# Products of the sampling weights one group further ahead, and the first tables' work in another order

## The chip, the cores and the metric

The kernel runs on one core of a Trainium2 chip. The metric is the device time of one execution, in microseconds; lower is better. Before the change the median of three runs is 1502.04 us (1500.31 to 1502.71).

## The reference, cut to what matters

Eight images x of 128 channels and 64 by 64 pixels, float32, go through two layers; each adds its output to its input.

```
x = x + relu(batchnorm(deform_conv(groupnorm(x))))       # layer 0
x = x + moe_conv(groupnorm(x))                           # layer 1
...
om   = conv3x3(x, off_w) + off_b                         # 27 channels: 18 offsets, 9 masks
py   = off_y + row - 1 + ky;   px = off_x + col - 1 + kx # per pixel and tap
val  = bilinear(x, py, px) * sigmoid(mask)               # 4 corners, weights (1-ly)(1-lx), ...
out  = einsum('bckhw,ock->bohw', val, w) + b
```

Layer 0, where the change lies, samples the normalised image at nine displaced points for each pixel and multiplies the samples with a 3 by 3 weight. Layer 1 mixes four 3 by 3 experts with weights chosen per image, and is untouched.

## The kernel before, in words

The function dense() does layer 0. All offsets of this input are under two pixels, so a sample is a sum over 5 by 5 neighbours, with a "tent" weight in y times one in x. The kernel turns the bilinear sampling into matrix products.

**Tiling.** An image is eight bands of eight rows, so there are 64 bands. In x a band is 15 tiles (NCOL) of four columns, handled in five groups (NGR) of three tiles. The pixels of a tile and its surround, 8 by 8 in each of two halves of the band, lie on the 128 partitions of xt.

**Work of one band g.** load_x and load_y fetch rows of the distance table in x (tabx, into one of three x_wts) and of the tent table in y (taby, into one of three y_wts), most of them by DMA from GpSimd's queue (lines 746 and 727): ten DMAs, 1.9 MB. spread (765, 768, 771) turns the distances into tents on ScalarE and clips them on VectorE. weights(n) (850) is the product s of the x and y weights for group n, counted over all bands, on VectorE; the pool a6 has five such buffers. pick (780) and pixels (809, 812) copy and transpose the normalised pixels into xt; share (823) copies the overlapping halves of xt, in four pieces on VectorE, ScalarE and SyncE's DMA. sample(n) (866, 876) multiplies xt with s on TensorE and copies the samples from PSUM on ScalarE. close(g) (892 to 899) fills the edges of the band's samples on VectorE. conv(g) (915, 923) runs the nine taps of the 3 by 3 product for the rows of band g and stores the result.

**Order.** The order is written out by hand: nothing is reordered, and each engine takes its instructions as the program emits them. Step g of the main loop emits, for the five groups q, first weights(5g+q+AHEAD) with AHEAD = 4 and then sample(5g+q); at q = 1, between them and the next, put_off(), which emits the statistics of the last convolution (996) and close(g-1). Then come the taps of conv(g-1). Between taps stand the pixels and spreads of band g+2, the loads and pick of band g+3, and ticks, which advance the tables of a coming image. So the first four products of a band are emitted in the step before, and its fifth at the head of its own step. load_x(g+3) writes the buffer that the products of band g read, so it waits for the fifth.

**Tables.** tables(b) is a generator that makes the tables of image b: normalisation, the offset convolution (392, 458), a store of its result by rows and columns to DRAM (525, 532), loads of it in another layout (570, 556), distances (616 to 631), the tents and masks (641 to 678), and stores to tabx (596) and taby (668). For image 0 it runs at the head with nothing beside it. Lines 535 to 541 pick and transpose the pixels of bands 0 and 1 there, between the offset convolution and the tables, and line 542 negates dw_sb. The first bands' tables are then stored ahead of the rest, and load_x(0) and load_y(0) follow them on several queues. The tables of image 1 (called later) are begun inside step 0.

**Clears.** The three y_wts tiles are set to zero once (262), since their loads fill only the parts that carry weights.

Of the kernel before, what the change touches and what calls it, by code (L numbers as in the profile page):

```python
# [65 lines left out]
def deform_moe_conv(  # L66
# [113 lines left out]
    def dense():  # L180

        with ExitStack() as st:
# [77 lines left out]
            y_wts = [a1.tile([P, T, 3, W, 3], F32, name=f"ywts{i}") for i in range(3)]  # L260
            for t in y_wts:
                nc.gpsimd.memset(t, 0.0)

# [10 lines left out]
            def pause(n):  # L274
                for _ in range(n):
                    yield
# [34 lines left out]
            def tables(b):  # L311
# [159 lines left out]
                if b < 2:  # L471
# [13 lines left out]
                    yield from block(0)  # L485
                    nc.vector.tensor_tensor(even, even, taken(0), ALU.add)
                    yield from block(3)
                    nc.vector.tensor_tensor(odd, odd, taken(3), ALU.subtract)
# [47 lines left out]
                if b == 0:  # L536
                    for g in range(2):
                        pick(g)
                        for _ in pixels(g, turn_odd=not g):
                            pass  # L540
                    pick(2)
                    nc.scalar.activation(dw_sb, dw_sb, AF.Copy, scale=-1.0)
                nc.vector.tensor_reduce(
                    most[:, b : b + 1], omr, AX.X, ALU.max, apply_absolute_value=True
                )
                yield from pause(8 if b == 1 else 16)
                by_row = rowwise[b].rearrange("(t k u) h w -> k h t u w", t=3, k=3)
# [13 lines left out]
                for k in range(3):  # L561
                    lo, hi = max(0, k - 1), min(H, H + k - 1)
                    places = [(slice(lo, hi), slice(lo + 1 - k, hi + 1 - k), k)]
                    if k == 2:
                        places.append((slice(0, 1), slice(0, 1), 0))
                    if k == 0:
                        places.append((slice(H - 1, H), slice(H - 1, H), 2))
                    for outs, parts, v in places:
                        for t in range(2):
                            nc.sync.dma_start(  # L570
                                out=raw_off[parts, v, t].rearrange("p (u w) -> p u w", u=3),
                                in_=by_row[k][outs, 2 * t],
                            )
                        by_column.append((k, outs, parts, v))
                if b:
                    yield from pause(27)
                for k, *where in by_column:
                    turned_in(nc.sync if b or k == 0 else nc.gpsimd, k, *where)
                if b == 0:
                    for piece in range(4):  # L580
                        share(1, piece, MOVES[piece])
                yield from pause((50, 17)[b] if b < 2 else 35)
# [116 lines left out]
                store_x(0, 2, nc.gpsimd)  # L699
                load_x(0, nc.gpsimd)  # L700
                for i in (0, 1, 2):
# [3 lines left out]
                for i in (3, 0, 4, 1, 2):  # L705
                    masked(i)
                    store_y(i, 1, soon)
                for k in range(Q):
                    for h in range(2):
                        load_y(0, k, (nc.sync, nc.gpsimd, nc.scalar, nc.gpsimd)[k % 4], (h,))  # L710
                store_x(2, 4, nc.scalar)
                store_y(0, NR, slice(4 * T, H))
                store_x(4, NROW, nc.sync)
                for _ in statistics(1):
                    pass
                for tiles in ((NCOL, NCOL + 1), (0, 3), (3, 9), (9, NCOL)):
                    spread(0, tiles)
# [71 lines left out]
            def pixels(g, turn_odd=False):  # L789
# [14 lines left out]
                for c0 in range(0, NCOL if turn_odd else EVEN, 4):  # L804
                    n = min(4, NCOL - c0)
                    pt = ps_c.tile([P, 4, P], F32, name="pt", tag="pc")
                    for c in range(c0, c0 + n):
                        one = picked[:, c] if c < EVEN else picked_odd[:, c - EVEN]
                        nc.tensor.transpose(  # L809
                            pt[:, c - c0], one.rearrange("p h x y -> p (h x y)"), ident  # L810
                        )
                    nc.scalar.copy(xts[g][:, c0 : c0 + n], pt[:, 0:n])  # L812
                    yield
# [152 lines left out]
            for _ in made:  # L966
                pass
            AHEAD = 4
            for n in range(AHEAD):
# [35 lines left out]
            for g in range(len(bands) + 1):  # L1005
# [6 lines left out]
                for q in range(NGR):  # L1012
                    if g < len(bands):
                        if g or q + AHEAD < NGR:
                            weights(g * NGR + q + AHEAD)
                        sample(g * NGR + q)
                        if g == 0 and q == 2:
                            for k in range(Q):
                                load_y(2, k, nc.gpsimd)
                    if g == 0 and q == 1:  # L1020
                        for _ in range(2):
                            while next(later) != BLOCK:
                                pass
                        for _ in range(8):
                            next(later)
# [662 lines left out]
```

## Time and profile before

| what | before |
| --- | --- |
| median of three runs | 1502.04 us |
| profiled execution's own time | 1501.57 us |
| its span in the profile | 1499.9 us |
| TensorE busy, share of the span | 1326.4 us, 88% |
| VectorE / ScalarE / GpSimd busy | 71% / 56% / 30% |
| mean granted TensorE clock | 0.943 |
| HBM traffic over the span | 150 GB/s |
| first sample on TensorE (line 866) starts | 74.90 us |
| last tap of layer 0 ends | about 1123 us |

A time is from the start of the span. A line such as L850 is line 850 of the kernel before; in the changed kernel the same statement stands some lines away. In a timeline a row is start, duration, engine, line, operation, output<-input, and in brackets the time that the engine stood idle before it and what it waited for. SPq, ACTq and POOLq rows are DMA issues from SyncE's, ScalarE's and GpSimd's queues. In a table of stretches each engine has its busy time[...].

### The profile page before, as it was taken

To read this page: it belongs to the slowest core of one execution; us is meant where nothing else is said; L and a number is where in the kernel's file an instruction comes from. 1 tells how busy PE (TensorE), PEld (TensorE's weight loads), DVE (VectorE), ACT (ScalarE), POOL (GpSimd) and SP (SyncE) were. 2 spreads that over 40 slices of the span, in tenths; PEclk is the share of its full clock that TensorE was granted. 3 is DMA by queue.
4 is the path that set the end of the run, shared out by engine and by line. 5 is a ranking of instruction groups with operands and counts; after the bars stand their busy time and mean duration, and the time that the engine had idled before them with its cause. 6 is when DMAs were issued, how large, how long until landed. Compare 5 with 4: busy or idle time off the path is not lost.

```text
span 1499.9 us, 21257 instructions
## 1 busy us (share of the span) xinstructions
PE 1326.4 (88%) x7561; PEld 753.6 (50%) x7561; DVE 1063.5 (71%) x2114; ACT 842.0 (56%) x1120; POOL 456.0 (30%) x752
## 2 busy tenths in 40 slices
PE   4179888998989999899999989999984999999998
PEld 1054456655655665565566556566552444444443
DVE  5556686677678668767866776766528888888882
ACT  2365665875686587568758756976734333222320
POOL 6253143333334233433423433344303010110100
PEclk9579999998999999999999989999996999999999
DMA  4496585976798597779859777789708344665411
GB/s 143 97 201 158 132 180 138 203 174 148 168 202 166 125 211 172 154 167 201 180 128 209 174 159 165 171 188 208 186 29 248 101 125 139 168 168 154 112 44 58
DMA packets 149544, 234.54 MB, mean 156 GB/s; under 512 B 101780, under 2 KB 105004, under 8 KB 139189
## 3 DMA queue, kind: packets, MB, share of 16 engines
q0 software_dynamic: 79376, 137.46, 43.5%
q1 hardware_dynamic: 69770, 95.22, 22.8%
q8 instruction: 61, 1.00, 0.3%
q14 instruction: 54, 0.44, 0.1%
q10 hardware_dynamic: 283, 0.42, 0.1%
HBM read 180.23 MB, written 45.35 MB: 150 GB/s over the span
## 4 chain that ended last, share of the span: by engine, by line
PE 35%; DMA 33%; DVE 12%; issue 9%; POOL 6%; ACT 3%; SPq 1%; DVEq 0%; POOLq 0%; ACTq 0%
DMA ywts<-taby 21%; PE pc L1600 12%; PE py L915 11%; PE pq L866 5%; POOL ywts L727 4%; PE pc L458 3%; DMA taby<-work 3%; DMA xwts<-tabx 2%; PE pt L809 2%; DMA xt<-xt 2%; DVE s L850 2%; DMA pad<-in_x_dram 1%; DMA x<-in_x_dram 1%; DVE xt L823 1%; DVE combo L425 1%
## 5 line engine op out<-in xcount | busy, mean ns | idle before, releaser
L915 PE MATMUL py<-samples,dw_sb 128*128 128x512 f32 (+3 forms) x1296 | 571.5, 575 | 13.2 <-ACT y L923 7.6
L727 POOL DMA_DIRECT2D ywts<-taby x512 | 316.1, 638 | 393.1 <-DMA xwts<-tabx 164.3
L866 PE MATMUL pq<-s,xt 64*128 64x144 f32 (+1 forms) x3840 | 297.1, 308 | 94.9 <-DVE s L850 69.8
L915 PEld LDWEIGHTS py<-samples,dw_sb 128*128 128x128 f32 x1296 | 233.2, 195 | 214.9 <-issue 173.7
L866 PEld LDWEIGHTS pq<-s,xt 64*128 64x128 f32 x3840 | 264.6, 195 | 146.8 <-issue 63.5
L876 ACT COPY samples<-pq 128x864 f32<-128x864 f32 (+1 forms) x320 | 282.1, 972 | 76.5 <-PE pq L866 76.5
L850 DVE TENSOR_TENSOR s<-xwts,ywts 128x432 f32<-128x432 f32 (+1 forms) x448 | 198.1, 497 | 24.0 <-PE pq L866 19.2
L1600 PE MATMUL pc<-v,u 128*128 128x512 f32 x384 | 175.9, 605 | 6.3 <-DVE v L1507 6.3
L1600 PE MATMUL pc<-v,wmix 128*128 128x512 f32 x384 | 174.2, 599 | 0.0
L771 DVE TENSOR_SCALAR xwts<-xwts 128x1152 f32<-128x1152 f32 (+2 forms) x128 | 96.0, 750 | 92.7 <-ACT xwts L765 86.3
L765 ACT ACTIVATE xwts<-xwts,place 128x1152 f32<-128x1152 f32 (+3 forms) x132 | 153.1, 1163 | 2.2 <-DMA xwts<-tabx 2.2
L746 POOL DMA_DIRECT2D xwts<-tabx x128 | 71.2, 563 | 241.3 <-DVE s L850 77.8
L1578 ACT ACTIVATE t<-pc,bmix 128x512 f32<-128x512 f32 x32 | 22.0, 687 | 189.2 <-PE pc L1600 100.5
L812 ACT COPY xt<-pt 128x512 f32<-128x512 f32 (+1 forms) x130 | 75.8, 583 | 89.7 <-PE pt L809 89.2
L1600 PEld LDWEIGHTS pc<-v,u 128*128 128x128 f32 x384 | 72.8, 193 | 93.5 <-issue 85.1
L1600 PEld LDWEIGHTS pc<-v,wmix 128*128 128x128 f32 x384 | 72.5, 190 | 91.3 <-issue 89.4
L780 DVE COPY picked<-pad 128x512 f32<-128x512 f32 x128 | 72.0, 604 | 60.4 <-PE pt L809 60.4
L809 PEld LDWEIGHTS pt<-ident,picked 128*128 128x128 f32 x512 | 66.3, 153 | 85.6 <-ACT xt L812 40.8
L923 ACT ACTIVATE y<-py,db_sb 128x512 f32<-128x512 f32 (+3 forms) x72 | 45.8, 636 | 110.1 <-PE py L915 103.0
L809 PE MATMUL pt<-ident,picked 128*128 128x128 f32 x512 | 85.8, 294 | 7.8 <-ACT xt L812 5.4
L823 DVE COPY xt<-xt 32x896 f32<-32x896 f32 x126 | 77.3, 614 | 1.5
L996 DVE BATCH_NORM_STATS2 ystats<-y 128x6 f32<-128x512 f32 (+3 forms) x72 | 44.6, 628 | 28.4 <-ACT y L923 28.4
(204 smaller groups left out, 1168.6 us busy)
## 6 DMA issues: line engine op xcount, KB each, us to landing
xwts<-tabx POOLq DMA_DIRECT2D x128, 576.0 KB, 8.2
pad<-in_x_dram SPq DMA_DIRECT2D x36, 512.0 KB
ywts<-taby POOLq DMA_DIRECT2D x126, 144.0 KB, 9.6
out_dram<-yo SPq DMA_DIRECT2D x32, 512.0 KB
ywts<-taby POOLq DMA_DIRECT2D x126, 108.0 KB, 9.1
yd<-y SPq DMA_DIRECT2D x48, 256.0 KB
ywts<-taby POOLq DMA_DIRECT2D x128, 72.0 KB, 8.6
pad<-yd SPq DMA_DIRECT2D x16, 512.0 KB
```

The lines of the kernel that those rows point to most:

```text
L727: engine.dma_start(out=y_wts[g % 3][HALF * h + k : HALF * (h + n) : Q, first : last + 1].rearrange("p r a b c -> p (r a b c)"), in_=bass.A ...
L765: nc.scalar.activation(some, some, AF.Abs, bias=columns[side])
L771: nc.vector.tensor_scalar(some, some, -1.0, 0.0, ALU.add, ALU.min)
L780: nc.vector.tensor_copy(picked[:, :, h], bass.AP(tensor=one.tensor, offset=one.offset, ap=[list(one.ap[0]), [Q, EVEN], [1, Q], [W, Q]],),)
L809: nc.tensor.transpose(pt[:, c - c0], one.rearrange("p h x y -> p (h x y)"), ident)
L812: nc.scalar.copy(xts[g][:, c0 : c0 + n], pt[:, 0:n])
L823: move(out=xts[g][rows, EVEN:].rearrange("p c n -> p (c n)"), in_=xts[g][rows, 1 - side : EVEN - side].rearrange("p c n -> p (c n)"),)
L850: nc.vector.tensor_tensor(s[:, :, 3 * at : 3 * (at + k)].rearrange("p m (c x) -> p m c x", x=3), by_x[:, :, c : c + k], by_y[:, :, w : w + ...
L866: nc.tensor.matmul(by_m[:, h, :, at : at + k], lhsT=xts[g][rows, c // 2 + EVEN * (c % 2)], rhs=s[rows, :, at : at + k], start=True, stop=True,
L876: nc.scalar.copy(bass.AP(tensor=one.tensor, offset=one.offset + first, ap=[list(one.ap[0]), [M * PLANE, 2], [PLANE, M], [WB + 1, 3], [1, w ...
L915: nc.tensor.matmul(py, lhsT=dw_sb[:, 3 * (2 - yy) + 2 - xx], rhs=samples[g % 2][:, m : m + 3 * n - 2 : 3, xx, 1 : W + 1], start=(i == 0), ...
L1600: nc.tensor.matmul(pc, lhsT=us[j][:, kx], rhs=vs[g][:, rows, kx : kx + W], start=(kx == 0), stop=(kx == 2),)
```

## The change

1. The three clears of y_wts leave the start of GpSimd's queue. The first is emitted on GpSimd inside the offset convolution of image 0, the other two on VectorE after the reduction of line 543.
2. Of the pixels at the head only band 0 stays in its place. Its transposes go to the three PSUM buffers of the samples (pq) and VectorE copies them out, where before they went through one buffer (pc) and ScalarE. Band 1's pixels and shares, pick(2) and the negation of dw_sb move behind the table stores and the statistics of image 1.
3. The ten loads by rows at the head, all on SyncE before, alternate between SyncE and ScalarE. load_x(0) moves from GpSimd to SyncE and behind the first five table stores; store_x(2, 4) from ScalarE to GpSimd.
4. The first part of image 1's tables (its mean and variance over groups) moves from step 0 to the head, in front of spread(0), with half of the eight ticks that followed it.
5. AHEAD becomes 5, still with five buffers, and sample(n) is emitted before weights(n+5). Step 0 emits no products within its loop; the five of band 1 come at its end.

```diff
--- before.py
+++ after.py
@@ -258,8 +258,6 @@
                 "p (c h x y) -> p c h x y", h=2, x=Q, y=Q
             )
             y_wts = [a1.tile([P, T, 3, W, 3], F32, name=f"ywts{i}") for i in range(3)]
-            for t in y_wts:
-                nc.gpsimd.memset(t, 0.0)
 
             samples = [a1.tile([P, 31, 3, WB], F32, name=f"samples{i}") for i in range(2)]
             dw_sb = a1.tile([P, TAPS, P], F32, name="dw_sb")
@@ -484,6 +482,8 @@
                         yield from combine(3)
                     yield from block(0)
                     nc.vector.tensor_tensor(even, even, taken(0), ALU.add)
+                    if b == 0:
+                        nc.gpsimd.memset(y_wts[0], 0.0)
                     yield from block(3)
                     nc.vector.tensor_tensor(odd, odd, taken(3), ALU.subtract)
                     yield
@@ -534,15 +534,15 @@
                         in_=om[32 * j + 9 : 32 * j + 18, 1],
                     )
                 if b == 0:
-                    for g in range(2):
-                        pick(g)
-                        for _ in pixels(g, turn_odd=not g):
-                            pass
-                    pick(2)
-                    nc.scalar.activation(dw_sb, dw_sb, AF.Copy, scale=-1.0)
+                    pick(0)
+                    for _ in pixels(0, turn_odd=True):
+                        pass
                 nc.vector.tensor_reduce(
                     most[:, b : b + 1], omr, AX.X, ALU.max, apply_absolute_value=True
                 )
+                if b == 0:
+                    for t in y_wts[1:]:
+                        nc.vector.memset(t, 0.0)
                 yield from pause(8 if b == 1 else 16)
                 by_row = rowwise[b].rearrange("(t k u) h w -> k h t u w", t=3, k=3)
 
@@ -567,7 +567,7 @@
                         places.append((slice(H - 1, H), slice(H - 1, H), 2))
                     for outs, parts, v in places:
                         for t in range(2):
-                            nc.sync.dma_start(
+                            (nc.sync if b or t == 0 else nc.scalar).dma_start(
                                 out=raw_off[parts, v, t].rearrange("p (u w) -> p u w", u=3),
                                 in_=by_row[k][outs, 2 * t],
                             )
@@ -576,9 +576,6 @@
                     yield from pause(27)
                 for k, *where in by_column:
                     turned_in(nc.sync if b or k == 0 else nc.gpsimd, k, *where)
-                if b == 0:
-                    for piece in range(4):
-                        share(1, piece, MOVES[piece])
                 yield from pause((50, 17)[b] if b < 2 else 35)
 
                 def moved(side, t, *dims):
@@ -697,7 +694,6 @@
                 nudged(sides[1])
                 distances_x()
                 store_x(0, 2, nc.gpsimd)
-                load_x(0, nc.gpsimd)
                 for i in (0, 1, 2):
                     for _ in tent(i):
                         pass
@@ -705,14 +701,27 @@
                 for i in (3, 0, 4, 1, 2):
                     masked(i)
                     store_y(i, 1, soon)
+                load_x(0, nc.sync)
                 for k in range(Q):
                     for h in range(2):
                         load_y(0, k, (nc.sync, nc.gpsimd, nc.scalar, nc.gpsimd)[k % 4], (h,))
-                store_x(2, 4, nc.scalar)
+                store_x(2, 4, nc.gpsimd)
                 store_y(0, NR, slice(4 * T, H))
                 store_x(4, NROW, nc.sync)
                 for _ in statistics(1):
                     pass
+                pick(1)
+                for _ in pixels(1):
+                    pass
+                for piece in range(4):
+                    share(1, piece, MOVES[piece])
+                pick(2)
+                for _ in range(2):
+                    while next(later) != BLOCK:
+                        pass
+                for _ in range(4):
+                    next(later)
+                nc.scalar.activation(dw_sb, dw_sb, AF.Copy, scale=-1.0)
                 for tiles in ((NCOL, NCOL + 1), (0, 3), (3, 9), (9, NCOL)):
                     spread(0, tiles)
 
@@ -803,13 +812,20 @@
                         )
                 for c0 in range(0, NCOL if turn_odd else EVEN, 4):
                     n = min(4, NCOL - c0)
-                    pt = ps_c.tile([P, 4, P], F32, name="pt", tag="pc")
+                    if turn_odd:
+                        pt = ps_q.tile([P, 2, CH], F32, name="pq")[:, 0].rearrange(
+                            "p (c n) -> p c n", n=P
+                        )
+                    else:
+                        pt = ps_c.tile([P, 4, P], F32, name="pt", tag="pc")
                     for c in range(c0, c0 + n):
                         one = picked[:, c] if c < EVEN else picked_odd[:, c - EVEN]
                         nc.tensor.transpose(
                             pt[:, c - c0], one.rearrange("p h x y -> p (h x y)"), ident
                         )
-                    nc.scalar.copy(xts[g][:, c0 : c0 + n], pt[:, 0:n])
+                    (nc.vector.tensor_copy if turn_odd else nc.scalar.copy)(
+                        xts[g][:, c0 : c0 + n], pt[:, 0:n]
+                    )
                     yield
 
 
@@ -965,7 +981,7 @@
                 pass
             for _ in made:
                 pass
-            AHEAD = 4
+            AHEAD = 5
             for n in range(AHEAD):
                 weights(n)
             HALVES = (0, EVEN), (EVEN, NCOL + 1)
@@ -1011,17 +1027,14 @@
                     tick()
                 for q in range(NGR):
                     if g < len(bands):
-                        if g or q + AHEAD < NGR:
+                        sample(g * NGR + q)
+                        if g:
                             weights(g * NGR + q + AHEAD)
-                        sample(g * NGR + q)
                         if g == 0 and q == 2:
                             for k in range(Q):
                                 load_y(2, k, nc.gpsimd)
                     if g == 0 and q == 1:
-                        for _ in range(2):
-                            while next(later) != BLOCK:
-                                pass
-                        for _ in range(8):
+                        for _ in range(4):
                             next(later)
                     if q == 1:
                         put_off()
```

## Prediction

> **What bounds the kernel now.** I read the page, then the table of stretches, then timelines where TensorE stood idle.
>
> ```profile
> PE 1326.4 (88%) x7561; PEld 753.6 (50%) x7561; DVE 1063.5 (71%) x2114; ACT 842.0 (56%) x1120; POOL 456.0 (30%) x752
> ...
> DMA ywts<-taby 21%; PE pc L1600 12%; PE py L915 11%; PE pq L866 5%; POOL ywts L727 4%; PE pc L458 3%; DMA taby<-work 3%; DMA xwts<-tabx 2%; PE pt L809 2%; DMA xt<-xt 2%; DVE s L850 2%; DMA pad<-in_x_dram 1%; DMA x<-in_x_dram 1%; DVE xt L823 1%; DVE combo L425 1%
> ```
>
> TensorE is the bound, idle 173 us; table loads lead the chain that ended last. Where is the idle time?
>
> ```profile
> 48.55:59.20 10.65, 0.00 (x0) 0.00 (x0) 10.27 (x22) 5.21 (x9) 1.86 (x3) 0.50 0.07 15
> 59.20:74.90 15.70, 0.00 (x1) 0.00 (x1) 7.36 (x16) 3.33 (x7) 6.83 (x13) 0.50 0.70 174
> 74.90:138.25 63.35, 51.90 (x341) 30.33 (x341) 38.89 (x71) 34.21 (x43) 28.54 (x49) 0.87 0.80 177
> 138.25:165.00 26.75, 26.14 (x173) 15.86 (x172) 14.65 (x31) 20.72 (x26) 11.47 (x20) 1.00 0.82 198
> 165.00:200.00 35.00, 23.48 (x151) 15.65 (x150) 29.06 (x66) 23.38 (x35) 4.69 (x6) 0.81 0.50 119
> 248.00:1125.00 877.00, 816.49 (x5618) 504.19 (x5618) 614.20 (x1252) 606.19 (x788) 317.52 (x525) 0.96 0.77 169
> ```
>
> (Columns: stretch, length, busy PE, PEld, DVE, ACT, POOL, clock, DMA share, GB/s.) No sample before 74.90; 11.5 us idle in bands 0 to 2; 11.5 us in 165 to 200; 60 us over the other 877. Two timelines, VectorE's head and the second image's tables:
>
> ```profile
> 46.15 1.22 DVE L543 TENSOR_REDUCE most<-om 128x1 f32<-128x1024 f32 x1
> ...
> 47.28 1.24 DVE L823 COPY xt<-xt 32x896 f32<-32x896 f32 x2
> 48.55 0.54 DVE L616 TENSOR_SCALAR combo<-combo,nudge 64x192 f32<-64x192 f32 x2
> ...
> 164.67 0.31 DVE L616 TENSOR_SCALAR combo<-combo,nudge 64x192 f32<-64x192 f32 x1 [7.45 <-DMA combo<-rowwise]
> 165.87 0.31 DVE L616 TENSOR_SCALAR combo<-combo,nudge 64x192 f32<-64x192 f32 x1 [0.89 <-DMA pad<-in_x_dram]
> 167.59 0.81 DVE L620 COPY combo<-combo 64x576 f32<-64x576 f32 x1 [1.41 <-DMA combo<-rowwise]
> ```
>
> L616 at 48.55 follows the copies without a wait: the first tables are late through other work queued ahead. At 164.67 the data is late, 9.75 us in all. A typical later stall:
>
> ```profile
> 344.08 1.41 DVE L850 TENSOR_TENSOR s<-xwts,ywts 128x432 f32<-128x432 f32 x4
> 344.83 2.05 PE L866 MATMUL pq<-s,xt 64*128 64x144 f32 x12 [3.28 <-DVE s L850]
> 345.40 0.69 DVE L996 BATCH_NORM_STATS2 ystats<-y 128x6 f32<-128x512 f32 x1
> 346.00 0.18 DVE L892 COPY samples<-samples 128x24 f32<-128x24 f32 x1
> 346.08 0.18 DVE L893 COPY samples<-samples 128x24 f32<-128x24 f32 x1
> 346.81 1.22 PE L915 MATMUL py<-samples,dw_sb 128*128 128x512 f32 x1
> ```
>
> The band's fifth sample group waits for its product; the convolution starts just after, and it needs L892 and L893 behind two products and a statistic.
>
> [...] No VectorE memset of this size is in the trace; GpSimd's took 2.02 us each. [...] here the 0.50 and 0.81 columns, and 2.05 us for the group after a 3.28 us gap, 1.13 after 2.01.
>
> **The change, part by part.**
>
> Clears. Three GpSimd memsets (5.9 us from 5.87) go. Eight statistics of 0.69 us from 6.11 could end at 11.6; they ended at 12.53. I take 0.9 us gained, bounds 0 and 0.9. One comes back on GpSimd after its last combination, hidden while it waits for L520; two on VectorE in the path to L616.
>
> First pixels. Before, from 34.65 to 48.52 VectorE's queue held two bands' pixels, each group of four transposes waiting for a ScalarE copy in one PSUM buffer (1.8 us a group), the reduction and two xt copies. Now: pick and odd copies to 36.5; four groups of at most 1.12 us without that wait, to 39.6; a last copy of 0.6, 40.2; reduction 1.2, 41.4; two memsets. Bounds for one: 1.36 us (L771 on as many elements)[...]; I take 2.45: 46.3. Less 0.9: 45.4, or **3.1 us earlier** (2.2 to 5.3). Row loads are the cover: ten on SyncE took 6.83 us from 38.39; five each on two queues end near 41.9, landed by about 44.
>
> To the first sample. L616 to the last masked tent is 10.2 us of VectorE work, unchanged. Row loads of x move to SyncE behind five table stores; they waited till 59.22 for the x store anyway, so nothing is lost. pick(1), its pixels, shares, pick(2) and the second image's mean (3.5 us of VectorE and waits) come behind statistics(1), where VectorE idled 6.4 us before 70.38. ScalarE now has y issues to 63.6, two copies behind transposes (68.5), a share 0.94 and the dw copy 1.17: 70.6, less 3.1 is 67.5. Data landed at 69.18, less 3.1 is 66.1. So the spread starts at 67.5, not 69.94: first sample at 72.4, **2.5 gained**.
>
> Bands 1 to 3. store_x(2,4) stood on ScalarE till 67.91; on GpSimd it waits for its first y load (issue near 57, landing 8.4 median): 65.6, then 0.6 each and 2 us landing: x(1) at 68.6 instead of 73.51. This load stream paces four bands (issues at 73.51, 82.85, 93.17, 104.32), so all move 4.9. Band 1: first sample to the fifth copy took 10.7, less 1.6 for the mean that now lies ahead, then spread 2.6, clip 1.36, product 0.8: 86.3 instead of 90.4. The 0.96 and 1.17 us waits on loads in bands 1 and 2 go with the stream. I take **5 us** by band 3 (2 to 9).
>
> Five ahead. With five buffers, product n+5 waits for sample n just as before (then n+4 before sample n): no new depth. What moves is each band's fifth product: from the head of its step to the end of the step before, ahead of the convolution. On VectorE, pick, the clips and the tables' steps queue behind its wait for the fifth sample, 0.84 us at most, where VectorE next idles about 1.7 us: nothing. It frees x and y buffers one convolution (8 us) earlier. GpSimd waited 77.8 us on these products. Band 7's loads went out at 153.36, beside the row loads of the second image (152.12 to 158.4). Now they precede them: those should land some 3 us after the last issue, not 9. Of 9.75 us waited, half: **5 us** (0 to 11.5, the whole idle time there).
>
> The late bands. The fifth group no longer waits: 14 such waits of 1.7 to 3.3 us after 248. But the convolution needs L893, now behind products 1 and 2 of the next band instead of the old fifth and the first: 36+6+36 columns instead of 36+6+36+6, some 0.15 us less. At 344 the convolution starts near 346.2 instead of 346.81; in the other two kinds (L893 was already last, 0.37 behind) 0.15 earlier. A wait takes the place of the wait. 5 x 0.6 + 9 x 0.15 = 4.3; the clock's slow stretch then lies in the convolution; I take **3** (-2 to 8).
>
> Sum: 5 + 5 + 3 = 13 us off 1501.57 (its span 1499.9 and 1.7 around it), 1488.6. The run lies 0.5 below the median 1502.04: 1489.
>
> **Rivals.** (a) Only the head gains: row loads of the second image wait for their own store (9.52 us landing) and not for the x and y loads, and the late bands are even: 5 + 1, 1496. For it: SyncE issues those loads over 6.3 us. Against: half that stretch's DMA load is GpSimd's. (b) Slower: the close lies behind a second product that waits for sample 1. In bands where VectorE was on time, L893 comes 0.55 us later; before it had 1.3 us to spare (255.47 against a convolution at 256.76). If that margin is gone, each of 56 bands pays 0.55: 31 less 13 gained, 1520. It decides from 24 such bands. Against: 0.7 us are left, and no wait on L893 shows in on-time bands. (c) The fifth product cures the stalls fully, because VectorE regains time: the 14 waits (33 us) halve: another 13, 1476. Against: VectorE's work ahead of the close is the same. (d) Nothing: the first sample is bound by loads that take as long: 1501.
>
> **Numbers.** Forecast 1489 (1483 to 1495): 0.50. (a) 1496: 0.20. (c): 0.12. (d): 0.07. (b): 0.11. About 0.2%, 3 us, can be told from no change. Faster 0.81, same 0.08, slower 0.11. The range 1476 to 1498 leaves out (b), (d) and the far side of (c), 0.2.
>
> **What would show it.** L616 near 45; first sample near 72; x(1) near 69; band 3 near 133; the wait on the second image's rows under 6 us and no 5 us gap after it; the wait "pq <- DVE s" nearly gone after 248 and "py <- DVE samples L893" grown to 2 us and more in its place. Wrong if row loads still land 9 us late, or if L893 waits show in every band.

## The result, and the profile after

The changed kernel takes 1483.07 us, median of four runs (1480.52 to 1485.34), against 1501.17 (1498.98 to 1502.71) before: ratio 0.988, 95% interval 0.9858 to 0.9902, so 18 us faster. The profiled execution took 1480.52 us, the lowest of its four, with a span of 1478.5, 21.4 less than before; the clock rose from 0.943 to 0.955. The page of the kernel after:

```profile
PE 1308.6 (89%) x7561; PEld 742.6 (50%) x7561; DVE 1068.6 (72%) x2120; ACT 838.0 (57%) x1116; POOL 470.2 (32%) x751
...
PE pc L1613 14%; PE py L931 12%; DMA ywts<-taby 8%; DMA xwts<-tabx 6%; PE pq L882 5%; POOL ywts L736 3%; DMA combo<-rowwise 3%; DMA combo<-colwise 3%; DMA taby<-work 3%; PE pc L456 2%; PE pt L823 2%; ACT xwts L774 2%; DVE s L866 2%; DMA x<-in_x_dram 1%; DMA pad<-in_x_dram 1%
```

TensorE ran the same 7561 matmuls in 17.8 us less busy time: most of the gain is not idle time removed. The loads of y tents fell from 21% of the chain to 8%. The same stretches as before, of the kernel after:

```profile
48.55:59.20 10.65, 0.00 (x0) 0.00 (x0) 10.48 (x21) 0.91 (x2) 5.65 (x11) 0.50 0.40 98
59.20:74.90 15.70, 7.75 (x58) 6.75 (x60) 8.30 (x21) 8.58 (x14) 7.14 (x12) 0.55 0.78 175
74.90:138.25 63.35, 49.88 (x330) 27.23 (x328) 38.61 (x68) 34.45 (x44) 32.08 (x53) 0.87 0.84 195
138.25:165.00 26.75, 26.15 (x170) 15.57 (x170) 18.95 (x41) 22.20 (x31) 5.57 (x10) 1.00 0.77 169
165.00:200.00 35.00, 28.15 (x166) 16.76 (x166) 28.69 (x66) 27.50 (x40) 11.89 (x17) 0.95 0.54 130
248.00:1125.00 877.00, 796.89 (x5538) 490.86 (x5538) 618.20 (x1268) 607.00 (x793) 335.82 (x529) 0.96 0.75 172
```

TensorE works 7.75 us between 59.20 and 74.90, where it did nothing before; 165 to 200 is idle for 6.9 us instead of 11.5. The last stretch now holds the start of layer 1, so it can't be set against that of before; I give layer 0's late bands by their own ends below. VectorE's timeline of the kernel after at the lines shown of before:

```profile
37.75 1.21 DVE L540 TENSOR_REDUCE most<-om 128x1 f32<-128x1024 f32 x1
39.39 1.98 DVE L545 MEMSET ywts<- 128x2304 f32 x1 [0.43 <-issue]
41.80 1.98 DVE L545 MEMSET ywts<- 128x2304 f32 x1 [0.43 <-issue]
43.69 0.41 DVE L613 TENSOR_SCALAR combo<-combo,nudge 64x192 f32<-64x192 f32 x2
...
157.05 0.54 DVE L613 TENSOR_SCALAR combo<-combo,nudge 64x192 f32<-64x192 f32 x2 [1.67 <-DMA combo<-rowwise]
```

The first nudge (L613, where the first tables begin) stands 4.86 us earlier; that of image 1 waits 1.67 us for its rows, where before three waits there came to 9.75.

**Where the 21.4 us lie.** I read the start of the first sample of bands from TensorE's timeline of each kernel (us):

| kernel | band 0 | 2 | 3 | 5 | 6 | 9 | 63 | span |
| --- | --- | --- | --- | --- | --- | --- | --- | --- |
| before | 74.9 | 114.0 | 138.2 | 165.4 | 188.4 | 252.6 | 1099.1 | 1499.9 |
| after | 70.5 | 110.0 | 135.7 | 162.9 | 178.8 | 241.6 | 1080.0 | 1478.5 |
| after, ahead by | 4.4 | 4.0 | 2.5 | 2.5 | 9.6 | 11.0 | 19.1 | 21.4 |
| e1_ahead_only | 75.2 | 116.7 | 140.9 | 168.1 | 184.0 | 249.1 | 1090.0 | 1489.9 |
| e2_head_only | 71.0 | 110.4 | 136.3 | 163.5 | 186.1 | 249.3 | 1090.7 | 1489.1 |
| e3_close_first | 70.5 | 109.4 | 132.3 | 159.5 | 174.7 | 237.6 | 1058.0 | 1457.3 |
| e8_hold_band6_loads | 70.9 | 112.9 | 138.7 | 165.8 | 188.3 | 253.0 | 1092.9 | 1490.5 |
| e9_head_routes_back | 74.9 | 111.3 | 133.7 | 160.9 | 176.9 | 240.1 | 1076.5 | 1474.5 |

So: 2.5 us by band 3, 7.1 from band 5 to 6 (the boundary between images 0 and 1), 8.1 from band 9 to 63, and the rest in layer 1 (2.3) and bands 6 to 9 (1.4). Layer 1's 2.3 I don't ascribe to the change: the tail after band 63 differs by as much between kernels that share it.

### The profile page after: what moved, and what is told of

It is laid out like the page before. It is cut to its first block, busy times and chain, and to the rows that moved or that the text cites. A ratio compares the mean times of both kernels' runs of the same rounds, so it can differ in the third digit from the quotient of the medians.

```text
span 1478.5 us, 21250 instructions
## 1 busy us (share of the span) xinstructions
PE 1308.6 (89%) x7561; PEld 742.6 (50%) x7561; DVE 1068.6 (72%) x2120; ACT 838.0 (57%) x1116; POOL 470.2 (32%) x751
## 4 chain that ended last, share of the span: by engine, by line
PE 36%; DMA 28%; issue 10%; DVE 10%; ACT 7%; POOL 6%; SPq 3%; DVEq 0%; POOLq 0%; ACTq 0%
PE pc L1613 14%; PE py L931 12%; DMA ywts<-taby 8%; DMA xwts<-tabx 6%; PE pq L882 5%; POOL ywts L736 3%; DMA combo<-rowwise 3%; DMA combo<-colwise 3%; DMA taby<-work 3%; PE pc L456 2%; PE pt L823 2%; ACT xwts L774 2%; DVE s L866 2%; DMA x<-in_x_dram 1%; DMA pad<-in_x_dram 1%
## 5 line engine op out<-in xcount | busy, mean ns | idle before, releaser
L931 PE MATMUL py<-samples,dw_sb 128*128 128x512 f32 (+3 forms) x1296 | 570.9, 574 | 57.0 <-DVE samples L909 49.3
L736 POOL DMA_DIRECT2D ywts<-taby x512 | 325.7, 652 | 363.9 <-DMA xwts<-tabx 156.5
L882 PE MATMUL pq<-s,xt 64*128 64x144 f32 (+1 forms) x3840 | 280.7, 300 | 25.3 <-ACT samples L892 21.1
L882 PEld LDWEIGHTS pq<-s,xt 64*128 64x128 f32 x3840 | 254.8, 189 | 73.0 <-issue 43.5
L826 ACT COPY xt<-pt 128x512 f32<-128x512 f32 x126 | 73.8, 586 | 134.6 <-PE pt L823 133.9
L755 POOL DMA_DIRECT2D xwts<-tabx x126 | 76.6, 614 | 228.1 <-ACT xt L826 76.0
```

The source lines that it names most:

```text
L736: engine.dma_start(out=y_wts[g % 3][HALF * h + k : HALF * (h + n) : Q, first : last + 1].rearrange("p r a b c -> p (r a b c)"), in_=bass.A ...
L755: engine.dma_start(out=x_wts[g % 3][HALF * h : HALF * h + HALF], in_=bass.AP(tensor=x_table[b].tensor, offset=x_table[b].offset + (2 * j + ...
L826: (nc.vector.tensor_copy if turn_odd else nc.scalar.copy)(xts[g][:, c0 : c0 + n], pt[:, 0:n])
L882: nc.tensor.matmul(by_m[:, h, :, at : at + k], lhsT=xts[g][rows, c // 2 + EVEN * (c % 2)], rhs=s[rows, :, at : at + k], start=True, stop=True,
L931: nc.tensor.matmul(py, lhsT=dw_sb[:, 3 * (2 - yy) + 2 - xx], rhs=samples[g % 2][:, m : m + 3 * n - 2 : 3, xx, 1 : W + 1], start=(i == 0), ...
```

## The experiments

My theory is that of the prediction: the head and the five ahead gain separately, the late waits are exchanged. The main rivals: the order of two emissions is what counts and not the depth; the boundary belongs to the head; the late gain is the run's.

**e1_ahead_only and e2_head_only: the change in two halves.** e1 is the kernel before with part 5 alone, e2 the kernel after without part 5.

```diff
                     if g < len(bands):
-                        if g or q + AHEAD < NGR:
-                            weights(g * NGR + q + AHEAD)
                         sample(g * NGR + q)
+                        if g:
+                            weights(g * NGR + q + AHEAD)
...
-            AHEAD = 4
+            AHEAD = 5
```

e1:

> The kernel before with part 5 alone: AHEAD = 5, the sample emitted ahead of the product; head unchanged. Theory: the fifth product's earlier place is what lets the second image's row loads land early and evens the late bands, so most of the gain is here: the wait of VectorE on those rows falls from 9.75 us to about 2, the idle time between 165 and 200 us falls by 6 to 7 us, and the median is 1491 (1488 to 1494). The waits on the product give way to waits on L893 of about the same length. Rival: the boundary gained only because the head ran ahead of the loads; then the rows stay about 9 us late here and the time is 1498 to 1501.

e2:

> The changed kernel with AHEAD = 4 and the product ahead of the sample, as before: the head's parts alone. Theory: first sample at 70.5 us as in the changed kernel, 3 to 4 us kept at band 3, rows of the second image late again (8 to 10 us of wait): 1497 (1495 to 1499). Rival: the head is what gained, and the products' place gives nothing: 1484 to 1490.

Measured, beside 1503.79 us for the kernel before: e1 1489.43 us, ratio 0.9912 (0.9882 to 0.9943); e2 1489.98, ratio 0.9917 (0.9886 to 0.9947). Each half alone is worth about the same, some 14 us by these medians. The whole is worth 18, so by the ratios (from 0.9912 or 0.9917 to 0.988) each adds only about 5 us once the other is there, with intervals as wide as that. The profiled executions gained 10.0 and 10.8 us beside the whole's 21.4; that looks like a plain sum, but it is single executions, and those of the kernel before lie anywhere from 1495.15 to 1509.66 us here. That the halves add is not shown. The table tells what each half does. From band 5 to 6 the kernel before takes 23.0 us and e2 22.6, e1 and the kernel after 15.9: the boundary belongs to part 5. e2 got the rival's time but not by its mechanism: VectorE still waited 6.83 us for image 1's rows. In its profile it gained 4 us at the first sample, 3 by band 9 and 5 more between bands 9 and 63, which I had not given to the head.

**e7_delay_at_head: what does a shift of the head alone do later?** The kernel before, with two clears more:

```diff
                 nc.vector.tensor_reduce(
                     most[:, b : b + 1], omr, AX.X, ALU.max, apply_absolute_value=True
                 )
+                if b == 0:
+                    for t in y_wts[1:]:
+                        nc.vector.memset(t, 0.0)
```

> The kernel before with two more clears of 128x2304 fp32 on VectorE behind the reduction that ends the offsets of image 0 (the tiles are cleared already, so nothing else differs): a plain delay at the head, to see whether the loop of bands keeps its length when only its start moves. By the clears' 1.98 us and 0.43 us ahead of each, the first sample moves from 74.9 to 78.5 to 79.7 us. Theory (the 5 us that the head-only kernel gained between bands 9 and 63 belong [...]to the run, not to the change): the time from band 9 to band 63 differs from 846.5 us by 2 us or more in this kernel too, and the total is anything from 1499 to 1509. Rival (a delay is only a delay): that stretch stays within 1 us of 846.5 and the total rises by 3.6 to 4.8 us, to 1506 to 1508.

Measured: 1503.47 us, ratio 1.0021 (1.0001 to 1.004). The first sample came at 80.1, 5.2 us late, somewhat over both expectations; bands 9 to 63 took 844.2 us, 2.2 less, and band 5 to 6 20.4 instead of 23.0: the theory's outcome. So the late stretch of one and the same loop varies by some 5 us: 846.4, 841.3 (e2) and 844.2. e2's late gain in the profile lies within that; only a difference beyond it may be given to part 5. What the head is worth in all stays open: by its interval e2's median is 8 to 17 us below that of the kernel before, and in its trace only some 3 us are gained ahead of band 9.

**e8_hold_band6_loads: why the boundary gained.** In the kernel after, band 6's loads went out at 120.82 us, before the store of image 1's rows; in the kernel before at 139.97, just ahead of that store. e8 holds them back until a product of band 4 is made:

```diff
                     if odd == 0 and part == 2:
+                        if g == 3:
+                            hold = a1.tile([1, 1], F32, name="hold")
+                            nc.gpsimd.tensor_copy(hold, ss[min(ss)][0:1, 0, 0:1])
                         load_x(g + 3, nc.gpsimd)
```

> The kernel after with one more GpSimd instruction, a copy of one element from the first product of band 4, ahead of the loads of band 6: they are then issued at about 138 us, beside the store of image 1's rows (138.4), as in the kernel before (140.0 beside 140.9), and not at 120.8. Theory (the boundary between the images gains because these loads no longer stand beside that store): the store lands after 9 to 10 us and not 5, the loads of the rows are issued at about 148 to 150 instead of 145.05, VectorE waits 5 to 8 us for rows again, band 5 to band 6 takes 20 to 24 us and not 15.9, and the time is 1487 to 1491 us. Rival (the fifth product alone covers the boundary, whatever the loads do): band 5 to band 6 stays at 15 to 17 us and the time within 1.5 us of 1482.

Measured: 1489.11 us, ratio 0.9927 (0.9906 to 0.9949), band 5 to 6 22.5 us. Its bands 2 to 5 came some 3 us later than in the kernel after, ahead of anything that the edit touches, so the step from 5 to 6 is the measure here and not the total. The store (L525), the row loads (L570) and the x loads of the bands, in the timelines of the queues; first the kernel before, then after, then e8 with VectorE's wait:

```profile
139.97 1.06 POOL L746 DMA_DIRECT2D xwts<-tabx  x2 [10.72 <-DVE s L850]
140.94 2.01 SPq L525 DMA_DIRECT2D rowwise<-om  x4
152.12 6.28 SPq L570 DMA_DIRECT2D combo<-rowwise  x10
```

```profile
120.82 1.08 POOL L755 DMA_DIRECT2D xwts<-tabx  x2
138.37 1.82 SPq L525 DMA_DIRECT2D rowwise<-om  x4
142.21 1.07 POOL L755 DMA_DIRECT2D xwts<-tabx  x2 [9.22 <-ACT samples L892]
145.05 10.86 SPq L570 DMA_DIRECT2D combo<-rowwise  x10
```

```profile
141.22 1.06 POOL L755 DMA_DIRECT2D xwts<-tabx  x2
141.32 1.58 SPq L525 DMA_DIRECT2D rowwise<-om  x4
151.78 7.04 SPq L570 DMA_DIRECT2D combo<-rowwise  x10
...
166.64 0.54 DVE L613 TENSOR_SCALAR combo<-combo,nudge 64x192 f32<-64x192 f32 x2 [7.56 <-DMA combo<-rowwise]
```

From the store's first issue to the row loads it takes 11.2 us with a band's loads issued within 1 us ahead of it, 6.7 without (as in e3 and e6), and 10.5 with them put back. The step from band 5 to 6 parts the runs: 20.4 to 23.0 us in four (before, e2, e7, e8), 15.1 to 16.0 in seven (after, e1, e3, e4, e9, e10, e11). With e8's edit, that shows the cause. The loads beside the row loads themselves (142.21 in the kernel after) matter less: the ten issues then take 10.86 us, and VectorE still waits only 1.67. Why the store takes longer beside a band's loads is not shown.

**e4_clears_on_gpsimd and e9_head_routes_back: what in the head pays.**

e4 puts the two clears on VectorE back on GpSimd, at the start:

```diff
             y_wts = [a1.tile([P, T, 3, W, 3], F32, name=f"ywts{i}") for i in range(3)]
+            for t in y_wts[1:]:
+                nc.gpsimd.memset(t, 0.0)
...
-                if b == 0:
-                    for t in y_wts[1:]:
-                        nc.vector.memset(t, 0.0)
```

> The changed kernel with the two clears that VectorE makes put back on GpSimd at the start. Theory: the two memsets (1.98 us each, with 0.43 us between) lie in front of the first distances at 43.69 us, but the loads of the rows land only at about 43, so taking them away moves that by at most 1 us, and GpSimd's clears cost up to 0.9 us at the start: 1482 to 1484. Rival: they were the bound, and the first distances start 4 us earlier: 1478 to 1480.

e9 puts part 3 back:

```diff
-                            (nc.sync if b or t == 0 else nc.scalar).dma_start(
+                            nc.sync.dma_start(
...
                 store_x(0, 2, nc.gpsimd)
+                load_x(0, nc.gpsimd)
...
-                load_x(0, nc.sync)
...
-                store_x(2, 4, nc.gpsimd)
+                store_x(2, 4, nc.scalar)
```

> The kernel after with the loads and stores of the head on the queues that they had before: all ten row loads of image 0 on SyncE, the x loads of band 0 on GpSimd right behind the first x store, the second x store on ScalarE. The pixels of bands 1 and 2, the transposes' place and the clears stay as after. Theory (with the clears taken out of VectorE's way it then waited 5.74 us for the rows, until 45.03: rows on two queues are what lets the first tables start at 43.69): the rows now end 2 to 3 us later, the nudge L613 starts at 45.5 to 47, the first sample at 72 to 73.5 instead of 70.55, the x loads of band 1 go out at 71 to 73.5 instead of 70.13, and the time is 2 to 5 us over the kernel after, 1485 to 1488. Rival (pixels off VectorE's path are the whole gain of the head): the first sample stays within 0.6 us of 70.55 and the time within 1.5 us of 1483.

Measured: e4 1482.10 us, ratio 0.9867 (0.9837 to 0.9897): no effect; without its clears VectorE waits 5.74 us for the rows, until 45.03. e9 1480.75, ratio 0.9881 (0.9852 to 0.991): no effect either, and 0.8 us below the rival's range. The nudge came at 44.07, after 0.31 us of waiting for the rows, 0.4 us later than in the kernel after and not 2 to 3. (In e4 the rows, on two queues, came only at 45.03; that two queues bring them sooner is not shown.) But the first sample came at 74.88, as late as before, which neither theory nor rival foresaw. Both read the first sample as the measure of the head, and it isn't: e9 is 2.0 us ahead of the kernel after at band 3, and no slower in all. What paces these bands may be the stream of x loads. Those of band 1 went out at 73.51 before, 70.13 after and 69.08 in e9: ahead by 3.4 and 4.4, against 2.5 and 4.5 at band 3. But that is argued and not shown: e8, up to there the same program as the kernel after, sent them at 70.81 and still began band 3 at 138.7, 3.0 us behind the kernel after and no earlier than before, 1.9 of it because the same matmuls of band 1 took longer. What one can see is one meeting with the stream, here in the timelines of ScalarE and TensorE of the kernel after:

```profile
88.29 1.25 ACT L774 ACTIVATE xwts<-xwts,place 128x1152 f32<-128x1152 f32 x1 [4.17 <-DMA xwts<-tabx]
...
90.78 2.60 ACT L892 COPY samples<-pq 128x1008 f32<-128x1008 f32 x3
...
91.85 3.49 PE L882 MATMUL pq<-s,xt 64*128 64x144 f32 x24 [4.18 <-ACT samples L892]
```

Band 2's spread waits 4.17 us for its x loads, band 1's sample copies stand behind it in ScalarE's queue, and TensorE waits 4.18 us for them: 3.2 us more than the 0.97 of before. e9, with its late first sample, has no such wait in band 1. Here an early band is paid back where it meets the stream. The pixels moved off VectorE's path are what is left as the head's gain; I didn't try them alone.

**e3_close_first, e5 and e6: the place of the close.** In the kernel after, the wait of a band's fifth product is gone and one for the close is there (waits of TensorE, 65 to 1110 us; total, times, longest), first before, then after:

```profile
PE pq L866 <- DVE s L850: 69.8, 19, 29.8
...
PE py L915 <- DVE samples L893: 3.8, 9, 0.8
```

```profile
74.90 3.49 PE L866 MATMUL pq<-s,xt 64*128 64x216 f32 x24 [29.81 <-DVE s L850]
```

```profile
PE py L931 <- DVE samples L909: 49.3, 19, 4.0
...
PE pq L882 <- DVE s L866: 4.3, 2, 3.6
```

The second view shows that 29.8 of the 69.8 us are the head's: TensorE's idle time ahead of its first sample, which in the kernel after is broken up by the transposes of band 1. Among the bands themselves there were 40.0 us at 18 times before, and 49.3 at 19 stand in their place: the waits did not get shorter.

e3 puts the statistics and the close ahead of both products; e5 does so in the kernel before, with four ahead; e6 moves the close alone.

```diff
                         sample(g * NGR + q)
+                        if q == 0:
+                            put_off()
                         if g:
                             weights(g * NGR + q + AHEAD)
...
-                    if q == 1:
+                    if q == 1 and g == len(bands):
                         put_off()
```

e3:

> The changed kernel with the statistics and the close of the last band emitted at q = 0, ahead of both products of the next band. Theory: in the late bands the convolution waits for the close only because two products (1.2 us) stand ahead of it on VectorE; with the close first the 19 waits on it (49 us) fall by about 1.2 us each, to some 28 us, and the time to 1468 (1462 to 1475), since the products are needed only a step later. Rival: VectorE is simply out of time in those bands and what it puts off comes back as a wait of the samples on the products in the next step: 1481 to 1485. Second rival: the statistics now wait for ScalarE's y copy at the head of the step and hold up VectorE in every band: slower than 1484.

e5:

> The kernel before, four products ahead, with one edit: the statistics and the close of the last band are put ahead of the first product of a band instead of after the second. Both theories agree that the close is what the convolution waits for in the kernel after, and differ on what five ahead is for. Theory (the two edits need each other): with four ahead the fifth sample of a band needs the first product made in that band, which now stands behind 0.7 us of statistics and 0.9 us of closing, and that wait (69.8 us at 19 boundaries before) can only stay or grow; the convolution's wait was 5.7 us and has nothing to give; 1495 to 1508 us, wait on the product 65 to 100 us. Rival (the place of the close is all, the count of products nothing): the time falls as in the kernel with both edits, 1475 to 1488 us.

e6:

> The kernel after with the close of the last band alone put right behind the first sample, the products behind it, and the statistics left where they are, behind the second product. Theory: the close is then reached one statistics instruction (0.68 us) earlier than in the kernel that moves both, where the convolution still waited 31.1 us at 19 boundaries; of these waits about 14 to 19 give 0.6 us each, so the time is 1448 to 1457 us and the wait 18 to 24 us. Rival (the close there waits for ScalarE's copy of the last sample, not for its place on VectorE): no gain over 1461 us, the wait 29 to 33 us.

Measured: e3 1460.96 us, ratio 0.9725 (0.9695 to 0.9756), better than both kernels, and below its expectation; the wait for the close fell to 31.1 us at 19 times. e5 1532.18, ratio 1.0209 (1.0172 to 1.0246): slower by more than the theory's upper end, the wait on the product 96.9 us at 29 times, or 67.1 at 28 without the head's. So five ahead has a worth that its own result hides: without it the close can't be first. e6 1465.68, ratio 0.976 (0.9725 to 0.9796), the wait 31.3 us: no better than e3, against the theory. The waits of TensorE for the close and for the mean of the coming image (L318, the first step of its tables; 0.9 us in the kernel after), in e3 and then in e6:

```profile
PE py L931 <- DVE samples L909: 31.1, 19, 3.3
...
PE pm L318 <- ACT xt L839: 7.8, 5, 1.6
```

```profile
PE py L931 <- DVE samples L909: 31.3, 18, 3.3
...
PE pm L318 <- DVE mv L306: 11.5, 6, 2.2
```

Three bands of an image have such waits. In two of them e6 did gain the 0.6 us (0.98 became 0.40 at band 21, 2.14 became 1.48 at band 23); in the third the wait grew by as much as they gained and more (1.66 became 3.26 at band 24), and the wait for the mean grew too. What is put off on VectorE there is waited for elsewhere, as e3's rival had it, though the time that it named for e3 was wrong.

**e10_middle_taps_first and e11_close_first_middle_taps: cover the close.** The middle column's taps don't read what L908 and L909 write:

```diff
                     for i in range(TAPS):
-                        yy, xx = divmod(i, 3)
+                        xx, yy = (1, 0, 2)[i // 3], i % 3
```

e10, from the kernel after:

> The kernel after with another order of the nine taps of each convolution: the three of the middle column first, which read samples that the two border copies of the close (L908, L909) do not write, then the left and the right column. Nothing is moved on VectorE. Theory (what is left at the head of most stalled bands is the wait for those copies, 49.3 us at 19 bands, up to 4.0 us each): three taps of about 0.55 us cover up to 1.7 us of each, some 25 us in all[...]: 1450 to 1462 us, the wait on the close under 25 us. Rival (the convolution is held by ScalarE's last copy of samples, of which the close is only the last in name): the wait goes over to ScalarE, and the time stays at 1478 to 1484 us.

e11, from e3:

> The kernel with the close put first (1461 us), and the taps of the middle column first as well. Theory: of the 31.1 us that the convolution still waited at 19 bands, 1.6 us in the mean, nearly all lies under three taps of 0.55 us: 1436 to 1448 us, and the wait on the close under 8 us. Rival (the clock is near full in that kernel already, and what stands behind the close then is VectorE itself): the products of the next band come late instead, and the time is 1455 to 1462 us.

Measured: e10 1463.84 us, ratio 0.9766 (0.9738 to 0.9794), the wait for the close 20.7 us at 6 times: slightly short of its expectation. e11 1455.7, ratio 0.9698 (0.9671 to 0.9726), the wait 13.9 at 6 times: the fastest kernel here, but not apart from e3 by their intervals, and at the rival's time. The clock was near full in e3 already, as the rival had it: 0.99 from 237.60 to 1058.00 us, against 0.97 from 241.60 to 1080.00 in the kernel after. It isn't the products that come late, as the rival had it (they are waited for twice, as in e3), but the coming image's mean: 13.3 us at 6 times. TensorE in the timeline of e3, then of e11, in the same two bands:

```profile
327.37 1.40 PE L931 MATMUL py<-samples,dw_sb 128*128 128x512 f32 x2 [2.07 <-DVE samples L909]
328.56 1.06 PE L823 MATMUL pt<-ident,picked 128*128 128x128 f32 x4
...
346.73 0.81 PE L931 MATMUL py<-samples,dw_sb 128*128 128x320 f32 x2 [1.65 <-DVE samples L909]
347.38 0.60 PE L823 MATMUL pt<-ident,picked 128*128 128x128 f32 x4
```

```profile
325.11 1.14 PE L931 MATMUL py<-samples,dw_sb 128*128 128x512 f32 x2
326.09 0.60 PE L823 MATMUL pt<-ident,picked 128*128 128x128 f32 x4
...
346.59 1.36 PE L931 MATMUL py<-samples,dw_sb 128*128 128x320 f32 x4 [2.64 <-DVE samples L909]
347.88 2.73 PE L456 MATMUL pc<-combo,offw_sb 128*32 128x256 f32 x24
```

In e3 the first wait of 2.07 us is followed by slow matmuls (four transposes 1.06 instead of 0.60), the second of 1.65 isn't. In e11 the first wait is gone and TensorE begins the next band's convolution 5.5 us earlier (341.18 instead of 346.73). But VectorE, busy without a gap with the coming image's tables, comes to L908 at 346.27, against 346.41 in e3; so the wait that comes is 2.64 us, with 24 matmuls in 2.73 us behind it that took 1.49 in e3. Most of a wait removed in one band comes back in the next, with the slow matmuls behind it.

**The late bands.** From the start of band 9 to that of band 63, before and then after (length, TensorE busy, and so on as above):

```profile
252.60:1099.10 846.50, 790.74 (x5489) 487.15 (x5488) 605.36 (x1231) 597.12 (x776) 317.52 (x525) 0.96 0.79 173
```

```profile
241.60:1080.00 838.40, 779.89 (x5487) 480.63 (x5486) 605.42 (x1229) 595.89 (x776) 327.26 (x515) 0.97 0.76 173
```

Idle is length less busy: 55.8 us before, 58.5 after. The exchange of waits made it no shorter; the same matmuls took 10.9 us less. A late stall in TensorE's timeline of the kernel before, then after:

```profile
477.59 2.05 PE L866 MATMUL pq<-s,xt 64*128 64x144 f32 x12 [3.27 <-DVE s L850]
479.57 2.07 PE L915 MATMUL py<-samples,dw_sb 128*128 128x512 f32 x2
481.44 1.06 PE L809 MATMUL pt<-ident,picked 128*128 128x128 f32 x4
482.29 1.68 PE L915 MATMUL py<-samples,dw_sb 128*128 128x512 f32 x2
```

```profile
463.04 2.07 PE L931 MATMUL py<-samples,dw_sb 128*128 128x512 f32 x2 [3.25 <-DVE samples L909]
464.90 1.06 PE L823 MATMUL pt<-ident,picked 128*128 128x128 f32 x4
465.76 1.14 PE L931 MATMUL py<-samples,dw_sb 128*128 128x512 f32 x2
```

The wait is as long, 3.27 and 3.25 us, but the slow matmuls behind it are fewer: the group's twelve (2.05 instead of 1.13) now run ahead of the wait at full speed (granted clock 1.00 from 457.50 to 459.80). The granted clock was 0.50 from 477.59 to 481.50 before, and from 463.00 to 464.90 after. Why the slow stretch ends sooner is not shown. Nor does a wait's length tell whether one follows: e3's wait of 2.07 us had one, and behind this one of 2.50 in the kernel after there is none:

```profile
355.23 0.81 PE L931 MATMUL py<-samples,dw_sb 128*128 128x320 f32 x2 [2.50 <-DVE samples L909]
355.89 0.60 PE L823 MATMUL pt<-ident,picked 128*128 128x128 f32 x4
```

Over all runs that share a loop, this stretch is 841.3 to 846.4 us with four ahead (before, e2, e7) and 836.4 to 841.0 with five and the close in its old place (after, e1, e4, e8, e9). Means are 844.0 and 839.1: about 5 us for part 5, though the two groups only just don't overlap. TensorE's busy time parts them better: 785.1 to 790.7 us against 776.0 to 782.0. So does the time from each band's first sample to its first tap, which I read from the same timelines and summed over bands 9 to 62: 284.3 to 288.3 us against 278.8 to 280.5, in the mean 7.5 less, of which some 2.5 come back behind the first tap. e3 has 820.4 us with 50.3 idle: 5.5 less idle than before, and 20.6 less in the matmuls.

## Why the prediction was right, point by point

The forecast was 1489 (1476 to 1498), the result 1483: direction right and the mechanism in the main, the sum of 13 short by 5 against the medians and by 8 against the profile it was made for.

**Clears.** 0.9 taken at the start; L488 came at 32.41 instead of 33.49, 1.1. The two on VectorE took 1.98 us each with 0.43 before each, so 2.41, near the 2.45 taken, which was my estimate and shown by no trace then. In e4, without them, VectorE waits for the rows instead and gains nothing.

**First pixels.** 3.1 taken, 4.86 measured: the four groups of copies took 2.37 us in all, from 35.47, where up to 1.12 for each and a last copy had been taken; so the reduction began at 37.75 and not at 40.2. The rows were named as the cover, to about 44; e4's 45.03 and e9's 44.07 are near that.

**First sample.** Forecast 72.4, measured 70.55, but e9 shows it to be the wrong yardstick.

**Bands 1 to 3.** Mis-sized: 5 taken, 2.5 measured, and even that is less than the 3.0 by which e8 and the kernel after, the same program up to there, differ. The store ahead of x(1) went out at 63.14, sooner than the 65.6 taken, but it was taken to land in 2 us and GpSimd waited 5.02 behind its last issue, so x(1) went out at 70.13 and not 68.6 (by the prediction's own figures nearer 69). The trace of before had this price: 3.7 us from the end of that store's issues at 69.84 to x(1) at 73.51. And the gain of a band was not checked against the spread of the next in ScalarE's queue: the 4.18 us wait at 91.85.

**Five ahead, the boundary.** 5 taken, 7.1 measured; e1 and e8 give it to part 5's earlier release of the buffers, as the prediction did. The pair of transfers was wrong: it had band 7's loads precede the row loads, but those stood beside them (142.21 and 145.05). Band 6's loads got out of the way of the store that comes before. Rival (a), the store as the bound, named the right transfer and the wrong conclusion: the store is not fixed at its 9.52 us.

**The late bands.** 3 taken, about 5 by the groups above (8.1 in the two profiles, part of which is the run's). The exchange of waits came as written, and rival (c), the stalls cured, fell: outside the head 49.3 us stand where 40.0 did. Counted from a band's first sample, the convolution starts 0.15 us sooner in most bands of two of the three stalled kinds (8.05 became 7.90 at band 21, 6.84 became 6.70 at band 24), as forecast, and 0.4 to 2.2 sooner in the third, where 0.6 was; there the last samples no longer run slow. But TensorE's idle time in the loop did not fall (55.8 us, then 58.5): the slow stretch, which the term left unsized, is the whole of the gain. That 3 came near 5 is in part luck.

**Rival (b)**, a close too late in every band, was not seen: 19 waits, no more bands than before. Its worry was sound all the same, with the other sign: the products ahead of the close cost time, and e3 gets some 22 us by undoing that (1460.96 against 1483.07; ratios 0.9725 and 0.988 to the kernel before).

What stays open: what the head is worth beyond the 3 us seen by band 9, how a 5.2 us delay at the head shrank to 2 at the end in e7, and what decides whether slow matmuls follow a wait.

## What to carry to other kernels

When one wait for a queue takes the place of another, look at once at what stands ahead of the new one in that queue: depth that lets you reorder (five ahead) may be worth little until the reordering is done. Count a stall as its idle time and the slow matmuls behind it. When a sum of waits is compared before and after, first take out the one long wait at the start. Judge an earlier start by when the following stages begin, not by the first instruction, and against how far executions of the same program differ there.

## What the runs showed of the hardware

- A VectorE clear of 128x2304 fp32 took 1.98 us (after, 39.39 and 41.80), with 0.43 us ahead of each that the trace counts as issue; one on GpSimd took 2.02 (before, L262).
- VectorE ran its instructions in the order in which they are emitted: with the close emitted behind the products it stands at 462.72 behind three of them from 460.94 (after), with the close emitted first at 405.11 ahead of those at 405.95 (e3).
- A TensorE wait of 2.07 us (e3, 327.37) was followed by matmuls at about half speed for some 3 us (two taps 1.92 at 329.42, 1.04 at 313.54), one of 1.65 (e3, 346.73) by none; but one of 2.50 (after, 355.23) was followed by none either (granted clock 1.00 from 355.23 to 359.00), so the length of a single wait doesn't decide.
- The loads that wait for a store of four DMAs of 108 KB went out 6.7 us after its first issue with no band's loads issued just ahead of it (after, e3, e6), 10.5 to 11.2 with one band's (before, e8).
